# Returning routed rows by scatter and plain load in a mixture-of-experts stage on one Trainium2 core

## The chip, the cores and the metric

The kernel runs on one core of one Trainium2 chip. A core has a matrix engine (TensorE, PE in the profile; its weight loads are shown as PEld), a vector engine (VectorE, DVE), a scalar engine (ScalarE, ACT), a general engine (GpSimd, POOL), and a synchronizing engine (SyncE, SP) that here issues plain DMAs. Each engine runs its own instruction list in order; semaphores order the engines among each other. GpSimd issues the indirect DMAs, which take one row address per partition from a tile in on-chip memory.

The metric is the device time in microseconds (us) of one execution. Several executions give a median. One further execution is recorded by the hardware profiler, and every duration below comes from that one.

## The reference

The input is 2048 tokens (8 sequences of 256) of width 256, all in float32. There are three layers, each followed by a residual sum and a layer norm.

```python
x = _layernorm(x + attention(x))          # 16 heads of 64, causal
x = _layernorm(x + slot_attention(x, ctx))  # 3 rounds of attention on ctx and a GRU cell
# third layer: a mixture of 8 experts beside a shared one
router_probs = softmax(x @ gate_w + gate_b)
expert_values, expert_indices = top_k(router_probs, k=2)
expert_values = expert_values / (sum(expert_values) + 1e-09)
moe_out = sum over the 2 chosen experts of expert_value * mlp(x, ew1[e], eb1[e], ew2[e], eb2[e])
x = _layernorm(x + x + mlp(x, sh_w1, ...) + moe_out)
```

Every `mlp` is 256 to 1024 to 256 with a tanh-approximated GELU. The change lies in the third layer.

## The kernel before

**Blocks.** Tokens are held in four blocks of 512 (`X[i]`, token-major, four groups of 128 partitions; `XT[i]`, feature-major). The first two layers fill the first 650 us and are not altered, except that the tiles `X[i]` become wider.

**Routing.** For each block, `route_rest(i)` computes the gate, the two best experts (`hot1`, `hot2`), their weights (`wt1`, `wt2`) and running counts. `place(i)` turns them into row numbers `slots[0]` and `slots[1]` in a table `xd` in device memory (2048 rows for each expert, and 256 spare), and issues eight indirect DMAs on POOL (L901): each of four groups of 128 tokens is scattered to its first and its second expert's rows. `tables()` turns the counts into a list of 23 tiles: 16 of two groups of 128 rows (pairs), 7 of one. `tei` holds each tile's expert, `tri` its first row.

**Expert tiles.** For each tile, SP loads the rows (`tile_fetch`, L1124, which waits for all the scatters), the first expert matrix (`tile_weights`) and the second (`tile_weights2`); `tile_turn` transposes the rows on TensorE and copies them out of PSUM on VectorE; `tile_up` and `tile_down` do the two matrix products. `tile_down` adds the bias on VectorE into `yo`, and SP stores `yo` into the same rows of a second table `yd` (L1172). Both tables are filled with zeros by two large DMAs early in the second layer (L535).

**Shared units.** The shared expert is cut into eight units of 256 tokens, numbered 0 to 7: `shared_up(u)` (TensorE, then GELU on ScalarE) and `shared_down(u)`, a generator that `parts(u)` steps twice. Its last step adds the result to `Z[i]` on VectorE (called z4, z5, ... below after the unit's number). Units below `SHARED_FIRST` run before the expert tiles, in the time in which routing and scatters go on; the others run after the tiles.

**The tail.** After the last tile, `fetch_back(i)` gathers each token's two rows from `yd` with eight indirect DMAs on POOL for each block (L1182); `take_back(i)` does eight VectorE instructions `Z += wt * y` (L1196); `finish(i, ...)` is the layer norm of a block (statistics L221 and L222, the root on ScalarE L130 and L131, three small VectorE steps, scaling L239) and the store to the output (L1200).

**Order.** From L1257 on, PE, ACT, DVE and POOL execute in the order in which the program is written. In the tile stage this holds for PE and ACT; there the framework orders DVE, POOL and SP itself. The tail before is:

```python
    shared_up(4); fetch_back(0); shared_up(5); fetch_back(1); take_back(0)
    parts(4); take_back(1); shared_up(6)
    nc.scalar.preload_act_table_set(LNEXP)
    finish(0); finish(1); fetch_back(2); parts(5); shared_up(7)
    nc.scalar.preload_act_table_set(LNEXP)
    take_back(2); finish(2); fetch_back(3); next(part[6]); take_back(3); next(part[6])
    finish(3, 0, half)   # then unit 7's two halves, each with its add and finish
```

Of the kernel before, what the change touches and what calls it, by code (L numbers as in the profile page):

```python
# [47 lines left out]
SHARED_FIRST = 4  # L48

NY = 16  # L50
# [11 lines left out]
def decoder_kernel(  # L62
# [47 lines left out]
    X = [act.tile([P, NSUB, D], F32, tag=f"X{i}", name=f"X{i}") for i in range(NBLK)]  # L110
# [42 lines left out]
    xd = tc.dram_tile([ROWS, D], F32, name="xd")  # L153
    yd = tc.dram_tile([ROWS, D], F32, name="yd")
# [376 lines left out]
    zeros = b1.tile([P, D], F32, name="zeros")  # L531
    nc.gpsimd.memset(zeros, 0.0)

    for table in (xd, yd):
        nc.sync.dma_start(  # L535
            table.rearrange("(p r) d -> p r d", p=P), zeros.unsqueeze(1).to_broadcast([P, ROWS // P, D])
        )
# [284 lines left out]
    def route_rest(i):  # L822
# [28 lines left out]
        def best(src, k, hot):  # L851
            top, first = s(f"top{k}"), s(f"first{k}")
            nc.vector.tensor_reduce(top, src, AX.X, ALU.max)
            tt(hot, src, wide(top), ALU.is_equal)
            tt(hot, hot, rankb, ALU.mult)
            nc.vector.tensor_reduce(first, hot, AX.X, ALU.max)
            tt(hot, hot, wide(first), ALU.is_equal)
            return top

        blk = ts(i, NSUB)  # L860
        top1 = best(pb, 1, hot1[:, blk, :])
        rest = t("rest")
        nc.vector.scalar_tensor_tensor(rest, hot1[:, blk, :], -2.0, pb, ALU.mult, ALU.add)
        top2 = best(rest, 2, hot2[:, blk, :])
# [9 lines left out]


    puts = []

    def place(i):
# [19 lines left out]
        for n in range(NSUB):  # L898
            for slot in slots:
                g = i * NSUB + n  # L900
                put = nc.gpsimd.indirect_dma_start(  # L901
                    out=xd[:, :],
                    out_offset=bass.IndirectOffsetOnAxis(ap=slot[:, g : g + 1], axis=0),
                    in_=X[i][:, n, :],
                    in_offset=None,
                )
                if puts:
                    tc.declare_no_dep(put.ins, group="puts", reason="other rows")
                tc.add_to_no_dep_group("puts", put.ins)
                puts.append(put)  # L910

    def tables():
# [81 lines left out]
        nc.vector.tensor_scalar(te, te, float(NE - 1), None, ALU.min)  # L994
        tei = fr.tile([P, NTILE], I32, name="tei")
# [116 lines left out]
    TI = {}  # L1112
# [7 lines left out]
    def tile_fetch(t):  # L1120

        row = nc.sync.value_load(tri[0:1, t : t + 1], min_val=0, max_val=ROWS - RT)
        xg = f2.tile([P, 2, D], F32, tag="xg", name=f"xg_{t}", bufs=4)[:, 0 : groups(t), :]
        load = nc.sync.dma_start(xg, rows_of(xd, row, t))  # L1124
        for put in puts:
            tc.add_manual_dep(
                load.ins,
                put.ins.name,
                mybir.DependencyInfo(mybir.DependencyClass.Sync, mybir.DependencyReason.DATA),
                reason="rows of the table",  # L1130
            )
        TI[t] = [row, xg]

    def tile_weights(t):
# [8 lines left out]
        TI[t] += [w1_sb, w2_sb, bt, b2t, e]  # L1143

    def tile_weights2(t):

        row, xgT, w1_sb, w2_sb, bt, b2t, e = TI[t]
        nc.sync.dma_start(w2_sb, ew2[ds(e, 1), :, :].rearrange("e (c p) d -> p (e c) d", p=P))
        nc.sync.dma_start(b2t, b2[ds(e, 1), :].to_broadcast([P, D]))

    def tile_turn(t):
# [8 lines left out]
        TI[t][1] = xgT  # L1160

    def tile_up(t):
        row, xgT, w1_sb, w2_sb, bt, b2t, e = TI[t]
        HT["t", t] = up(w1_sb, bt, xgT, f"t{t}")

    def tile_down(t):
        row, xgT, w1_sb, w2_sb, bt, b2t, e = TI.pop(t)
        n = groups(t)
        po = down(w2_sb, HT.pop(("t", t)), f"t{t}", groups=n)
        yo = f2.tile([P, 2, D], F32, tag="yo", name=f"yo_{t}")[:, 0:n, :]  # L1170
        tt(yo, po[:, 0:n, :], b2t.unsqueeze(1).to_broadcast([P, n, D]), ALU.add)
        nc.sync.dma_start(rows_of(yd, row, t), yo)  # L1172
# [3 lines left out]
    def fetch_back(i):  # L1176

        for n in range(NSUB):
            for j, slot in enumerate(slots):
                g = i * NSUB + n  # L1180
                y = f2.tile([P, D], F32, tag="y", name=f"y_{g}_{j}", bufs=NY)
                nc.gpsimd.indirect_dma_start(  # L1182
                    out=y,
                    out_offset=None,
                    in_=yd[:, :],
                    in_offset=bass.IndirectOffsetOnAxis(ap=slot[:, g : g + 1], axis=0),
                )
                Y[g, j] = y

    def take_back(i):  # L1190

        for n in range(NSUB):
            g = i * NSUB + n
            for j, wt in enumerate((wt1, wt2)):
                z = Z[i][:, n, :]
                nc.vector.scalar_tensor_tensor(z, Y.pop((g, j)), wt[:, g : g + 1], z, ALU.mult, ALU.add)  # L1196
# [31 lines left out]
    for t in TILES[:2]:  # L1228
        tile_fetch(t)
    tile_weights(TILES[0])  # L1230
    tile_weights2(TILES[0])
    for u in range(2, SHARED_FIRST):
        shared_up(u)
        if u == SHARED_FIRST - 1:
            tile_fetch(TILES[2])
            tile_weights(TILES[1])
            tile_turn(TILES[0])
        parts(u)
    for u in range(SHARED_FIRST, nunit):
# [19 lines left out]
    shared_up(4)  # L1259
    fetch_back(0)  # L1260
    shared_up(5)
    fetch_back(1)
    take_back(0)
    parts(4)
    take_back(1)
    shared_up(6)
    nc.scalar.preload_act_table_set(LNEXP)
    for i in range(2):
        finish(i, 0, NSUB)
    fetch_back(2)  # L1270
    parts(5)
# [4 lines left out]
    fetch_back(3)  # L1276
    next(part[6])
    take_back(3)
    next(part[6])
# [74 lines left out]
```

## Time and profile before

| what | value |
|---|---|
| median of 3 runs | 1054.72 us (1053.62 to 1055.31) |
| the profiled execution's own time | 1057.97 us |
| its span | 1056.3 us, 13679 instructions |
| mean granted TensorE clock | 0.991 of full speed |
| PE busy | 1031.2 us |
| DVE, ACT, POOL busy | 484.3, 466.6, 257.4 us |

The span runs from the first to the last recorded instruction or transfer, so the execution's own time is 1.67 us longer. The stages on the time axis of the span: attention to about 373 us, slot attention to about 650 us, routing with shared units 0 to 3 to 714 us, expert tiles to 994 us, the tail to the end. Lines of the timeline give the start, the duration, the engine and source line, the operation with its output and inputs, the count of merged instructions, and in brackets the idle time of that engine before it with what ended it.

### The profile page before, as it was taken

The page shows a single profiled execution, that of the slowest core. Times are in us where ns is not written, and L with a number is a line of the kernel's source. Part 1 is how long each engine was busy: PE and PEld are TensorE (multiplying, and loading weights), DVE is VectorE, ACT ScalarE, POOL GpSimd, SP SyncE. Part 2 cuts the span into 40 slices and gives each one's busy share as a digit, 9 for nine tenths or more (in the row PEclk, how much of TensorE's full clock was granted, in tenths as well). Part 3 has the DMA queues.
Part 4 walks back from the last instruction along what each step waited for, and adds up shares of the span by engine and source line. Part 5 has one row for each costly group of instructions (what it writes and reads, how often), then busy time and mean ns, then how long its engine had stood idle before and what let it go on. Part 6 is the DMA issues. An engine that isn't in the chain of part 4 may idle for free. (4 is left out here: it accounts for less than half of the span.)

```text
span 1056.3 us, 13679 instructions
## 1 busy us (share of the span) xinstructions
PE 1031.2 (98%) x4686; PEld 714.5 (68%) x4686; DVE 484.3 (46%) x1378; ACT 466.6 (44%) x1156; POOL 257.4 (24%) x280
## 2 busy tenths in 40 slices
PE   9999999899898999999999999999999999999997
PEld 5444555455444865565655657888888888888886
DVE  4677766677678462444443568630110100101057
ACT  3567766665667123555545535223222222222232
POOL 2333423542367122112112003430000000000172
PEclk9999999899899999999999999999999999999999
DMA  9754434343345489990000001155766676665143
GB/s 325 122 86 83 83 67 74 60 76 68 68 90 102 118 286 348 348 311 1 1 0 1 1 0 44 63 167 194 253 208 237 205 255 213 221 223 171 64 120 105
DMA packets 195492, 144.24 MB, mean 137 GB/s; under 512 B 107551, under 2 KB 185951, under 8 KB 195423
## 3 DMA queue, kind: packets, MB, share of 16 engines
q1 hardware_dynamic: 191263, 132.88, 44.8%
q0 software_dynamic: 3072, 8.39, 2.5%
q10 hardware_dynamic: 1088, 2.10, 0.5%
q8 instruction: 37, 0.61, 0.2%
q14 instruction: 32, 0.26, 0.1%
HBM read 72.70 MB, written 45.48 MB: 112 GB/s over the span
## 5 line engine op out<-in xcount | busy, mean ns | idle before, releaser
L1063 ACT ACTIVATE hT_t<-ph_t,bt 128x256 f32<-128x256 f32 (+1 forms) x184 | 71.3, 438 | 202.6 <-issue 139.1
L348 ACT ACTIVATE sc<-sc,nmax 128x128 f32<-128x128 f32 (+1 forms) x256 | 113.3, 443 | 106.5 <-DVE nmax L335 106.2
L363 POOL TENSOR_TENSOR sc<-sc,sums 128x256 f32<-128x256 f32 (+1 forms) x128 | 104.0, 833 | 185.0 <-DVE sums L360 185.0
L1054 PE MATMUL ph_t<-xgT,w 128*128 128x256 f32 (+1 forms) x736 | 140.3, 348 | 0.8 <-ACT hT_t L1063 0.8
L1068 PE MATMUL pf_t<-w,hT_t 128*128 128x256 f32 x624 | 138.3, 379 | 0.0
L1054 PEld LDWEIGHTS ph_t<-xgT,w 128*128 128x128 f32 x736 | 123.8, 190 | 15.0 <-ACT hT_t L1063 1.0
L748 PE MATMUL gate<-XT,whh_sb 128*128 128x512 f32 x288 | 133.8, 593 | 0.0
L1068 PEld LDWEIGHTS pf_t<-w,hT_t 128*128 128x128 f32 x624 | 116.9, 190 | 15.0
L1182 POOL DMA_INDIRECT y<-yd,slot x32 | 31.0, 967 | 308.1 <-PE ph_s L1054 298.7
L748 PEld LDWEIGHTS gate<-XT,whh_sb 128*128 128x128 f32 x288 | 54.2, 189 | 48.5 <-issue 46.2
L391 DVE COPY pT<-turned 128x1536 uint16<-128x1536 uint16 x64 | 86.3, 1348 | 1.1 <-DMA turned<-planes 1.1
L335 DVE CUSTOM_DVE_ANT_0 sc<-pp,mask 128x128 f32<-128x128 f32 (+1 forms) x256 | 76.0, 353 | 19.5 <-PE pp L323 19.0
L757 PEld LDWEIGHTS gate<-at,G 120*128 120x128 f32 x288 | 54.5, 189 | 29.9 <-issue 23.2
L1159 DVE COPY xgT<-xg 128x512 f32<-128x512 f32 (+1 forms) x23 | 14.0, 611 | 131.7 <-PE xg L1157 131.7
L379 ACT COPY planes<-sc 128x1536 uint16<-128x1536 uint16 x48 | 70.5, 1470 | 5.9 <-POOL sc L363 5.8
L605 DVE TENSOR_TENSOR yo<-pf_t,b2t 128x512 f32<-128x512 f32 (+1 forms) x23 | 14.0, 610 | 127.9 <-PE pf_t L1068 127.9
L757 PE MATMUL gate<-at,G 120*128 120x256 f32 x288 | 72.2, 379 | 0.4 <-DVE at L605 0.4
L298 PE MATMUL pq<-XT,wq_sb 128*128 128x512 f32 x128 | 66.4, 643 | 0.0
L298 PE MATMUL pq<-XT,wk_sb 128*128 128x512 f32 x128 | 63.3, 617 | 0.0
L308 PE MATMUL pv<-wv_sb,XT 128*128 128x512 f32 x128 | 59.7, 594 | 0.0
L405 PE MATMUL po<-pT,v 128*64 128x256 f32 (+1 forms) x512 | 57.1, 345 | 1.0 <-DVE sums L360 1.0
L421 PE MATMUL py<-wo_sb,ot 128*128 128x256 f32 x256 | 57.9, 381 | 0.0
(209 smaller groups left out, 1430.9 us busy)
## 6 DMA issues: line engine op xcount, KB each, us to landing
w<-in_ew_dram SPq DMA_DIRECT2D x46, 1024.0 KB, 5.5
xd<-zeros SPq DMA_DIRECT2D x1, 16640.0 KB, 51.2
yd<-zeros SPq DMA_DIRECT2D x1, 16640.0 KB, 99.4
xg<-xd SPq DMA_DIRECT2D x16, 256.0 KB, 5.2
yd<-yo SPq DMA_DIRECT2D x16, 256.0 KB, 5.6
b2t<-in_b_dram SPq DMA_DIRECT2D x23, 128.0 KB, 5.2
sh<-in_sh_w_dram SPq DMA_DIRECT2D x2, 1024.0 KB, 6.7
X<-in_x_dram SPq DMA_DIRECT2D x3, 512.0 KB, 11.6
```

What stands on the lines that cost most here:

```text
L298: nc.tensor.matmul(pq, w[:, dc, ts(pr, P)], XT[i][:, dc, :], start=dc == 0, stop=dc == DC - 1)
L308: nc.tensor.matmul(pv, XT[i][:, dc, ts(n, P)], wv_sb[:, dc, ts(hf, 512)], start=dc == 0, stop=dc == DC - 1)
L335: nc.vector.tensor_tensor_reduce(out=sc[:, h, seg[t]], in0=pp[h][:, seg[t]], in1=mask[:, seg[t]], scale=-(HD**-0.5), scalar=3.0e38, op0=AL ...
L348: nc.scalar.activation(sc[:, h, seg[t]], sc[:, h, seg[t]], AF.Exp, scale=-1.0, bias=nmax[:, t, h : h + 1], accum_out=sums[:, t, h : h + 1],)
L363: nc.gpsimd.tensor_tensor(sc[:, :, seg[t]], sc[:, :, seg[t]], sums[:, t, :].unsqueeze(2).to_broadcast([P, 2, w]), ALU.mult,)
L379: nc.scalar.copy(planes, words)
L391: nc.vector.tensor_copy(pT.rearrange("p h c -> p (h c)").bitcast(U16).rearrange("p (n w) -> p w n", w=2), turned.rearrange("p (w c) q -> p ...
L748: nc.tensor.matmul(pg[:, oc, :], whh_sb[:, dc, o], XT[i][:, dc, :], start=dc == 0, stop=not given and dc == DC - 1,)
L757: nc.tensor.matmul(pg[:, oc, ts(bi, S)], G[:, BPB * i + bi, o], AT_[p][:, bi, :], start=not hidden, stop=not hidden or bi == BPB - 1,)
L1054: nc.tensor.matmul(ph[:, a, 0:w], w1_sb[:, dc, ts(c, P)], rhs[:, dc, :], start=dc == 0, stop=dc == DC - 1,)
L1063: nc.scalar.activation(hT[:, c, 0:w], ph[:, a, 0:w], AF.Gelu_apprx_tanh, bias=bias[:, c : c + 1])
L1068: nc.tensor.matmul(po, hT[:, c, ts(a, P)], w2_sb[:, c, :], start=c == 0, stop=c == FC - 1)
```

## The change

Tokens get an address of their own. The tiles `X[i]` become 16 columns wider (`XW`, row width `DW` = 272). Column 256 holds twice the token number plus 1; column 257 holds the rank of the token's first expert. The scatters into `xd` carry these columns along. In `tile_turn`, three small VectorE instructions make from them the row of the new table `yd` to which each result belongs: `2 * (token + 1) + j`, where j is 1 for the first expert and 0 for the second; unused rows of a tile go to rows of their own behind the tokens' rows. `tile_down` then issues one or two indirect DMAs on POOL in place of SP's store. `fetch_back(i)` is one plain load of 1 MB on SP, which waits for all these scatters. `yd` is not filled with zeros any more.

In `place`, a small `memset` of the last column of groups n and n+1 stands on POOL after the two scatters of group n. The scatters of group n read that column, so POOL waits for their end before it goes on with group n+1.

`SHARED_FIRST` goes from 4 to 5, the turning of the first tile comes after `parts` of the last early unit, and the tail is written anew.

```diff
-SHARED_FIRST = 4
+SHARED_FIRST = 5
+DW = D + 16
-    X = [act.tile([P, NSUB, D], F32, tag=f"X{i}", name=f"X{i}") for i in range(NBLK)]
+    XW = [act.tile([P, NSUB, DW], F32, tag=f"X{i}", name=f"X{i}") for i in range(NBLK)]
+    X = [t[:, :, 0:D] for t in XW]
...
-    xd = tc.dram_tile([ROWS, D], F32, name="xd")
-    yd = tc.dram_tile([ROWS, D], F32, name="yd")
+    xd = tc.dram_tile([ROWS, DW], F32, name="xd")
+    yd = tc.dram_tile([2 * (NT + 1) + P * (2 * NPAIRT + NSINGLE), D], F32, name="yd")
+    for i in range(NBLK):
+        nc.gpsimd.memset(XW[i][:, :, D:DW], 0.0)
+        nc.gpsimd.iota(XW[i][:, :, D], pattern=[[2 * P, NSUB]], base=2 * (i * BLK + 1), channel_multiplier=2, ...)
...
-    for table in (xd, yd):
-        nc.sync.dma_start(
-            table.rearrange("(p r) d -> p r d", p=P), zeros.unsqueeze(1).to_broadcast([P, ROWS // P, D])
-        )
+    nc.sync.dma_start(
+        xd.rearrange("(p r) d -> p r d", p=P), zeros.unsqueeze(1).to_broadcast([P, ROWS // P, DW])
+    )
...
-        top1 = best(pb, 1, hot1[:, blk, :])
+        top1 = best(pb, 1, hot1[:, blk, :], XW[i][:, :, D + 1])
...
                 put = nc.gpsimd.indirect_dma_start(
                     out=xd[:, :],
...
-                    in_=X[i][:, n, :],
+                    in_=XW[i][:, n, :],
...
+            if n + 1 < NSUB:
+                nc.gpsimd.memset(XW[i][:, n : n + 2, DW - 1 : DW], 0.0)
...
         nc.vector.tensor_copy(xgT, pt)
-        TI[t][1] = xgT
+        to = f2.tile([P, 2], I32, tag="to", name=f"to_{t}", bufs=6)
+        own, none = (f2.tile([P, 2], F32, tag=tag, name=f"{tag}_{t}")[:, 0:n] for tag in ("own", "none"))
+        g = 2 * t if n == 2 else NPAIRT + t
+        nc.vector.scalar_tensor_tensor(
+            own, xg[:, :, D + 1], tile_rank[:, t : t + 1], xg[:, :, D], ALU.is_equal, ALU.add
+        )
+        nc.vector.scalar_tensor_tensor(none, xg[:, :, D], 0.0, unused[:, g : g + n], ALU.is_equal, ALU.mult)
+        tt(to[:, 0:n], own, none, ALU.add)
+        TI[t][0:2] = to, xgT
...
-        yo = f2.tile([P, 2, D], F32, tag="yo", name=f"yo_{t}")[:, 0:n, :]
+        yo = f2.tile([P, 2, D], F32, tag="yo", name=f"yo_{t}", bufs=3)[:, 0:n, :]
         tt(yo, po[:, 0:n, :], b2t.unsqueeze(1).to_broadcast([P, n, D]), ALU.add)
-        nc.sync.dma_start(rows_of(yd, row, t), yo)
+        for k in range(n):
+            put = nc.gpsimd.indirect_dma_start(
+                out=yd[:, :],
+                out_offset=bass.IndirectOffsetOnAxis(ap=to[:, k : k + 1], axis=0),
+                in_=yo[:, k, :],
+                in_offset=None,
+            )
...
     def fetch_back(i):
-        for n in range(NSUB):
-            for j, slot in enumerate(slots):
-                g = i * NSUB + n
-                y = f2.tile([P, D], F32, tag="y", name=f"y_{g}_{j}", bufs=NY)
-                nc.gpsimd.indirect_dma_start(out=y, in_=yd[:, :], in_offset=... slot[:, g : g + 1] ...)
+        y = f2.tile([P, NSUB, 2, D], F32, tag="y", name=f"y_{i}")
+        load = nc.sync.dma_start(
+            y, yd[2 * (i * BLK + 1) : 2 * ((i + 1) * BLK + 1), :].rearrange("(n p j) d -> p n j d", p=P, j=2)
+        )
+        after(load, outs)
...
     tei, tri = tables()
-    for t in TILES[:2]:
-        tile_fetch(t)
+    tile_fetch(TILES[0])
     tile_weights(TILES[0])
     tile_weights2(TILES[0])
+    for t in TILES[1:3]:
+        tile_fetch(t)
     for u in range(2, SHARED_FIRST):
         shared_up(u)
-        if u == SHARED_FIRST - 1:
-            tile_fetch(TILES[2])
-            tile_weights(TILES[1])
-            tile_turn(TILES[0])
         parts(u)
+    tile_weights(TILES[1])
+    tile_turn(TILES[0])
...
-    shared_up(4)
-    fetch_back(0)
+    for i in range(2):
+        fetch_back(i)
     shared_up(5)
-    fetch_back(1)
-    take_back(0)
-    parts(4)
-    take_back(1)
     shared_up(6)
     nc.scalar.preload_act_table_set(LNEXP)
     for i in range(2):
+        take_back(i)
+        fetch_back(i + 2)
+    parts(5)
+    for i in range(2):
         finish(i, 0, NSUB)
-    fetch_back(2)
-    parts(5)
+    parts(6)
     shared_up(7)
     nc.scalar.preload_act_table_set(LNEXP)
     take_back(2)
     finish(2, 0, NSUB)
-    fetch_back(3)
-    next(part[6])
     take_back(3)
-    next(part[6])
     finish(3, 0, half)
```

The `y` tiles are two of 8 KB per partition where there were sixteen of 1 KB.

## The prediction, made before the changed kernel was run

> **What bounds the kernel now.** I read the page's busy times first, then TensorE's waits, then the timeline of the two places that the change touches: the start of the expert tiles and the tail.
>
> ```profile
> PE 1031.2 (98%) x4686; PEld 714.5 (68%) x4686; DVE 484.3 (46%) x1378; ACT 466.6 (44%) x1156; POOL 257.4 (24%) x280
> ```
>
> ```profile
> PE pp L321 <- DVE qk L300: 13.3, 11, 2.9
> ...
> PE ph_t L1054 <- ACT hT_t L1063: 0.8, 1, 0.8
> ```
>
> The first line is the page's, the others are TensorE's waits (total us, times, longest). TensorE is busy for 98% of the span. Only one line of waits is over 1.2 us in all, and it lies in attention, which the change leaves alone. In the tile stage TensorE waits once, for 0.8 us. So everything that the change takes off SP and POOL in the tiles was hidden, and TensorE's work is the same after as before: one shared unit moves from behind the tiles to ahead of them. A gain can come only from what follows TensorE's last product.
>
> ```profile
> 720.82 0.60 PE L1157 MATMUL xg<-ident,xg 128*128 128x128 f32 x4
> 721.45 0.69 DVE L1159 COPY xgT<-xg 128x512 f32<-128x512 f32 x1 [6.66 <-PE xg L1157]
> 722.24 7.14 PE L1054 MATMUL ph_t<-xgT,w 128*128 128x256 f32 x32 [0.83 <-ACT hT_t L1063]
> ```
>
> This is that one wait: the second tile is turned directly ahead of its own `tile_up`. The label names ACT, but the copy on DVE (721.45 to 722.14) is what ends last.
>
> ```profile
> 1008.06 7.07 PE L1068 MATMUL pf_s<-sh,hT_s 128*128 128x256 f32 x32
> ...
> 1015.17 0.69 DVE L605 TENSOR_TENSOR Z<-Z,pf_s 128x512 f32<-128x512 f32 x1 [4.89 <-PE pf_s L1068]
> 1015.77 3.23 DVE L1196 SCALAR_TENSOR_TENSOR Z<-y,wt,Z 128x256 f32<-128x256 f32 x7
> ...
> 1020.29 0.42 DVE L221 BATCH_NORM_STATS2 bnst<-Z 128x6 f32<-128x256 f32 x1
> ...
> 1026.70 0.41 DVE L221 BATCH_NORM_STATS2 bnst<-Z 128x6 f32<-128x256 f32 x1
> ...
> 1031.40 0.68 DVE L605 TENSOR_TENSOR Z<-Z,pf_s 128x512 f32<-128x512 f32 x1
> 1032.00 3.75 DVE L1196 SCALAR_TENSOR_TENSOR Z<-y,wt,Z 128x256 f32<-128x256 f32 x8
> 1035.67 0.42 DVE L221 BATCH_NORM_STATS2 bnst<-Z 128x6 f32<-128x256 f32 x1
> 1035.68 13.98 PE L1068 MATMUL pf_s<-sh,hT_s 128*128 128x256 f32 x64
> ...
> 1040.50 3.75 DVE L1196 SCALAR_TENSOR_TENSOR Z<-y,wt,Z 128x256 f32<-128x256 f32 x8
> ...
> 1044.16 0.68 DVE L605 TENSOR_TENSOR Z<-Z,pf_s 128x512 f32<-128x512 f32 x1
> ...
> 1047.88 0.41 DVE L605 TENSOR_TENSOR Z<-Z,pf_s 128x256 f32<-128x256 f32 x1
> ...
> 1050.48 0.41 DVE L605 TENSOR_TENSOR Z<-Z,pf_s 128x256 f32<-128x256 f32 x1
> ```
>
> This is the tail. Two things are to be seen. DVE runs in the written order: at 1015.17 it had waited 4.89 us for unit 4's product, with `take_back(1)` queued behind. And from 1020.29 DVE hardly pauses: `finish(0)`, `finish(1)`, z5, `take_back(2)`, and so on to 1053.16 (the last scaling). TensorE is done at 1049.66. So at the end two engines finish nearly together: TensorE through four units in 55.4 us (994.25 to 1049.66), DVE 3.5 us later. The gathers on POOL feed DVE, but after 1020 DVE is the slower of the two.
>
> **The change part by part, against the profiled execution (span 1056.3).**
>
> *Scatters in pairs.* The trace has no such wait. The nearest row is the scatter's own landing:
>
> ```profile
> xd<-X,slot POOLq DMA_INDIRECT x32, 2.4
> ```
>
> A pair takes 0.96 + 0.31 us up to the second scatter's start (rows of L901), then 2.4 us to land and about 0.3 us for the memset: 4.0 us. The last pair of a block has no wait (2.5 us). POOL starts `place(2)` at 679.5 as before; twice 3 x 4.0 + 2.5 ends at 708.5, the last lands near 710. SP's first fetch waits for that, as does the first tile's load of weights behind it: fetch at about 710, landed after 5.4 us (L1124's median; longest 7.8) at 716 to 718; weights issued by 713, landed by 722 even with the longest landing of L1141 (9.0). TensorE needs the rows after three units: 685.76 + 3 x 13.86 = 727.3 (a unit is half of 713.91 - 685.76 - 0.44). Cost: 0, and 9 us of cover. The six waits decide only if each landing takes 1.5 us more (3.9; the longest in the trace is 3.6). The second tile's weights, now behind `parts(4)` in the program, stand behind two more fetches on SP and issue by 716, 18 us ahead of their use. `place(0)` and `place(1)` end by about 653 and 675, ahead of POOL's next work. The Trainium skill speaks against the wider rows: "DMA: Bandwidth & Descriptors", section "How a descriptor splits into AXI transactions", says that a transfer that does not begin on a 256-byte boundary fetches unused bytes. Rows of 1088 bytes begin 0, 64, 128 or 192 bytes off, so a row takes some 37 beats for 32, an estimate of 16% more: landing 2.8 for 2.4, fetch 6.3 for 5.4. No row here shows it, and with it the rows arrive 3 us later, still under cover; the sum is the same by both.
>
> *First tile turned behind `parts(4)`.* A new wait on TensorE: before, 6.9 us of unit 3 lay over the copy. Lower bound 0.83 us (the row above); upper bound 1.5, if DVE does z4 (0.60 to the next start) in full ahead of the copy: z4 starts 0.2 after the product, the copy at 0.8, TensorE at 1.6, less 0.44 of transposes that existed before. I take 1.15. Behind the copy, three small DVE instructions (near 0.2 us each) are before `yo`; DVE is busy 26.7 of 279 us in the tile stage, so they cost nothing, and neither does the one added to `tables()`, which ends at 693, before the scatters.
>
> *Results scattered.* 39 indirect DMAs on POOL (16 x 2 + 7) of 1.27 us each stand in an engine that is idle for 298.7 us there; SP loses 23 stores and the waits for `yo` ahead of its weight loads. TensorE had no wait for weights, so the gain is 0; if POOL fell behind, three `yo` tiles (some 30 us) would cover it.
>
> *Zeros.* 16.6 MB are not written, 1.0 MB are added. They run from 373 to 473 us; TensorE is busy for 100.55 of the 101 us from 374 to 475: 0.
>
> *Start.* Eight small POOL instructions; POOL idles 10.8 us there. If the first loads of `X` had to wait for them, up to 2.4 us would be lost. I take 0: two loads into interleaved columns of `wq_sb` leave 1.1 us apart though each takes 4 us to land, so the order is kept by columns, not by whole tiles.
>
> *The tail.* Let E be TensorE's end of the tiles: 994.25 now, 994.25 + 13.86 + 1.15 = 1009.3 after. From E: the last `yo` 0.2 to 0.9, two scatters, the second landed at about 4.8; a load of 1 MB takes 5.5 (row of `w`), so block 0 is there at 10.3, block 1 at about 13.3. Two `take_back` (3.7 each) end by 18.7. Then DVE stands before z5 until TensorE has done units 5 and 6 up and 5 down: E + 20.9, exactly as z4 now (1015.17 - 994.25). From there, with durations from start to start in the rows above:
>
> z5 0.60; `finish(0)` and `finish(1)` 4.70 each (1026.70 to 1031.40); z6 0.60; `take_back(2)` 3.67; `finish(2)` 4.83 (1035.67 to 1040.50); `take_back(3)` 3.66; `finish(3, 0, half)` 3.01 (1044.87 to 1047.88); unit 7's halves 2.60 and 2.68. Sum 31.05.
>
> DVE therefore ends at E + 51.95, while TensorE has only three units and ends at E + 41.6. The overhang behind TensorE grows from 3.5 to 10.4 us: the moved unit was the cover of `finish(0)` and `finish(1)`, and those still come after a wait for TensorE. Last instruction 1009.3 + 51.95 = 1061.2, and the output's landing as before (1056.3 - 1053.16 = 3.1): span 1064.4, 8.1 us more. The profiled time would be 1057.97 + 8.1 = 1066.1. The median of the runs is 3.25 under the profiled time; I carry the difference over: 1054.72 + 8.1 = 1062.8.
>
> *The gathers gone.* A second rule weighs here. Of DVE's passes, eight `take_back` instructions beside gathers took 3.75 us (1032.00) and eight without any (1040.50, POOL done at 1038.6) took 3.75 too. The Trainium skill, "GPSIMD Engine Reference", section "Key points", says that GpSimd shares its SBUF interfaces with VectorE, in contention with instructions of two SBUF inputs, which these are. By the rule, each of some 15 gathers after 1020.3 could hold DVE for up to its 0.95 us, and without them DVE would gain up to 14 us (an estimate), enough to turn the sign. By the row the gain is 0, and I take the row. What is seen to stretch is the gather (1.13 for 0.95).
>
> **The rivals.**
>
> *A, DVE sets the end as above:* 1062.8, own range 1060.5 to 1065.5. Chance 0.76.
>
> *B, also a late supply:* scatters or loads land later than their rows. At the first tile this takes 9 us of lateness; in the tail `take_back(1)` has only 2.2 us of slack before z5, so 4 us more there, from 23 tiles' scatters and two loads of 1 MB at once, puts 2 us on top, and a late first tile more: 1064 to 1070. Against it: longest landings of 3.6 and 9.0. Chance 0.10.
>
> *C, the wait for z5 does not bind:* DVE does the two `finish` before z5, from E + 17.7. Then z5 follows at E + 27.1, and the rest (31.05 - 9.40) ends at E + 48.9: 5 us more than before, 1059.7. Against it: the 4.89 us wait before z4 shows the written order. Chance 0.05.
>
> *D, not slower:* DVE's own instructions get shorter because POOL leaves the shared interface. Place: the 31 us from z5 on. It decides from 8.1 us on, a quarter of that chain; then TensorE's end plus 2.8 sets the time, 1054.72 + 1.15 - 0.7 = 1055.2, and any further gain has to come from shorter waits in the first layers. Against it: 3.75 with gathers, 3.75 without. Chance 0.09 with all unseen causes of that kind.
>
> **How the numbers follow.** The prediction is A's 1062.8. The range runs from C's neighbourhood to the lower half of B: 1059.5 to 1066.5. About 0.2% (2.1 us) is what a measurement of this kernel can tell from no change. A, B and C lie over it; D gives 0.05 to no difference and 0.04 to faster.
>
> **What would show it.** Right: TensorE's last product near E + 41.6 with DVE's last scaling 10 us behind; DVE idle 2 us ahead of z5; `finish(0)` starting after z5; POOL empty in the tail; one new TensorE wait of about 1.2 us before the first tile; the last scatter of `place(3)` near 710. Wrong: `take_back` or the statistics shorter than 0.48 and 0.40 us; TensorE idle before the first tile for several us; block 1 landing after E + 17.

## The result, and the profile after

The changed kernel took 1062.67 us against 1054.87 us for the kernel before in the same comparison: ratio 1.0072, 95% interval 1.0054 to 1.0091. It is slower by 7.8 us; 8.1 had been forecast. One of the five executions of the changed kernel took 2748.68 us; it is left out of the ratio, and its cause is not known. The profiled execution took 1062.67 us, its span is 1061.0 us.

Two marks make the two traces comparable: the first product of `place(1)`, and E, TensorE's end of the tiles. In the trace of before they are

```profile
656.29 0.30 PE L884 MATMUL place<-cur,upper 128*128 128x32 f32 x2
994.25 13.98 PE L1054 MATMUL ph_s<-XT,sh 128*128 128x256 f32 x64
```

and in the trace of after

```profile
653.31 0.30 PE L902 MATMUL place<-cur,upper 128*128 128x32 f32 x2
1006.29 13.98 PE L1089 MATMUL ph_s<-XT,sh 128*128 128x256 f32 x64
```

(the row of E is the first product behind the tiles). The first mark comes 2.98 us earlier in the trace of after. This is not the change's doing: slot attention already begins 2.96 us earlier (370.21 against 373.17), behind attention, in which the granted clock was 0.97 between 150 and 200 us and between 250 and 300 us where it was 0.93 in the trace of before. It also shows that leaving out 16.6 MB of zeros behind that point gave nothing that can be seen. From that mark to E it is 337.96 us before and 352.98 after; from E to the end of the span 62.05 before and 54.71 after. So +15.02 and -7.34, together +7.7 us.

The start of the tiles, from the timeline of after (start, duration, engine and line, operation, and in brackets the engine's idle time before it with what ended it):

```profile
717.35 7.07 PE L1103 MATMUL pf_s<-sh,hT_s 128*128 128x256 f32 x32
724.25 0.60 PE L1186 MATMUL xg<-ident,xg 128*128 128x128 f32 x4
724.46 0.69 DVE L615 TENSOR_TENSOR Z<-Z,pf_s 128x512 f32<-128x512 f32 x1 [4.17 <-PE pf_s L1103]
725.06 0.68 DVE L1188 COPY xgT<-xg 128x512 f32<-128x512 f32 x1
725.80 7.17 PE L1089 MATMUL ph_t<-xgT,w 128*128 128x256 f32 x32 [0.94 <-DVE xgT L1188]
```

The first tile is now turned behind unit 4's second product. VectorE is asked for z4 and for the copy at once, does z4 first, and TensorE waits 0.94 us. It is the only wait over 0.3 us that TensorE has gained behind the first mark; the 0.8 us ahead of the second tile are as before.

The tail, from the timeline of after:

```profile
1016.96 7.42 DVE L1242 SCALAR_TENSOR_TENSOR Z<-y,wt,Z 128x256 f32<-128x256 f32 x16 [9.77 <-DMA y<-yd]
1027.22 0.69 DVE L615 TENSOR_TENSOR Z<-Z,pf_s 128x512 f32<-128x512 f32 x1 [2.83 <-PE pf_s L1103]
1027.82 0.42 DVE L232 BATCH_NORM_STATS2 bnst<-Z 128x6 f32<-128x256 f32 x1
...
1041.08 7.07 PE L1103 MATMUL pf_s<-sh,hT_s 128*128 128x256 f32 x32
...
1046.22 3.75 DVE L1242 SCALAR_TENSOR_TENSOR Z<-y,wt,Z 128x256 f32<-128x256 f32 x8
...
1057.76 0.41 DVE L250 TENSOR_SCALAR Z<-Z,mv,rstd 128x256 f32<-128x256 f32 x1
```

E is 1006.29. VectorE is done with both first `take_back` at 1024.4 and stands idle for 2.83 us until TensorE has produced z5 at E + 20.9. Behind that wait lie `finish(0)` (from 1027.82), `finish(1)` and all the rest. TensorE ends its last unit at 1048.15 (E + 41.9), VectorE at 1058.2 (E + 51.9): 10 us lie behind TensorE's last product, where there were 3.5 before.

### The profile page after: what moved, and what is told of

Same layout as the page of the kernel before. It is cut to its first block, busy times and chain, and to the rows that moved or that the text cites. A ratio compares the mean times of both kernels' runs of the same rounds, so it can differ in the third digit from the quotient of the medians.

```text
span 1061.0 us, 13689 instructions
## 1 busy us (share of the span) xinstructions
PE 1027.9 (97%) x4686; PEld 711.8 (67%) x4686; DVE 493.1 (46%) x1448; ACT 466.6 (44%) x1156; POOL 266.9 (25%) x308
## 5 line engine op out<-in xcount | busy, mean ns | idle before, releaser
L1214 POOL DMA_INDIRECT yd<-yo,to x39 | 37.4, 959 | 271.3 <-DVE yo L615 266.5
L346 DVE CUSTOM_DVE_ANT_0 sc<-pp,mask 128x128 f32<-128x128 f32 (+1 forms) x256 | 76.0, 353 | 18.7 <-PE pp L334 18.2
L1193 DVE SCALAR_TENSOR_TENSOR own<-xg,tile_rank 128x2 f32<-128x2 f32 (+1 forms) x23 | 5.1, 221 | 123.8 <-DMA xg<-xd 123.8
## 6 DMA issues: line engine op xcount, KB each, us to landing
X<-in_x_dram SPq DMA_DIRECT2D x3, 512.0 KB, 11.9
```

The source lines that it names most:

```text
L346: nc.vector.tensor_tensor_reduce(out=sc[:, h, seg[t]], in0=pp[h][:, seg[t]], in1=mask[:, seg[t]], scale=-(HD**-0.5), scalar=3.0e38, op0=AL ...
```

## The experiments

Two theories were to be told apart. **A**, the prediction's: VectorE's written order in the tail sets the end; the fifth early unit is missing there as cover. **S**, formed after the first experiments: where GpSimd issues many indirect DMAs without a gap, the other engines run out of instructions.

The experiments ran on a chip (chip 2 in the results) on which the kernel before is slower: 1092 us in the first two sets, 1086 in the last. Whether the comparison above ran on the same chip is not recorded. So each kernel is compared with the kernel before in its own set, and by ratios with the unaltered changed kernel below. The traces of one set are single executions, so small differences between them count only where a wait in the trace accounts for them. Expectations of the first two sets know only theory A and what could stand against it then.

**The changed kernel, unaltered, on that chip**

> The changed kernel itself, beside the kernel before on one chip. Theory A: some 8 us slower (ratio 1.0072 in the first measurement). In the first set of experiments the kernel before took 1092 us where it had taken 1055, and the four variants 1064 to 1072 with one stall of 5 to 6 us of TensorE in unit 2's product that the first trace of the changed kernel does not have. If that set's chip only adds that stall to all kernels, the changed kernel is 1072 to 1073 there, so that its four variants lie 2.7, 0.9, 8 and 3.7 us lower as theory A has them.

Measured: 1071.54 us, ratio to the kernel before 0.9819 (0.9802 to 0.9837). The sign is turned: here the change is 1.8% faster. All ratios below are to be held against this 0.982. TensorE stops once that it did not in the first comparison, in the second product of unit 2:

```profile
698.68 6.20 PE L1103 MATMUL pf_s<-sh,hT_s 128*128 128x256 f32 x20 [4.84 <-ACT hT_s L1098]
```

**The kernel before, unaltered, one execution**

> The kernel before, for its trace on the chip of this set. If this chip is like the one of the first measurement: the trace as before, 1053 to 1058. If it is like the one of the first set of experiments: near 1092, and the trace shows TensorE waits of some 30 us in all that name what the kernel before does there and the variants do not; candidates are the second table's zeros (16.6 MB on the queue from 373 to 473 us) and the start of the expert tiles.

Measured: 1089.53 us, span 1087.8. TensorE's waits in this trace, those with the shared units' products (total, times, longest):

```profile
PE ph_s L1054 <- issue: 11.7, 8, 2.2
PE ph_s L1054 <- ACT hT_s L1063: 11.1, 3, 10.0
```

Neither line is in the trace of before that the prediction used. "issue" means that the engine waited for nothing that the profile shows. The timeline of the same trace shows where:

```profile
692.51 1.99 PE L1054 MATMUL ph_s<-XT,sh 128*128 128x256 f32 x8 [0.92 <-ACT hT_s L1063]
704.51 3.78 PE L1054 MATMUL ph_s<-XT,sh 128*128 128x256 f32 x8 [10.00 <-ACT hT_s L1063]
...
1039.16 0.58 PE L1054 MATMUL ph_s<-XT,sh 128*128 128x256 f32 x1 [1.52 <-issue]
1041.25 0.59 PE L1054 MATMUL ph_s<-XT,sh 128*128 128x256 f32 x1 [1.51 <-issue]
1043.35 0.59 PE L1054 MATMUL ph_s<-XT,sh 128*128 128x256 f32 x1 [1.51 <-issue]
```

The first stop ends 2.9 us after the 16 scatters of `place(2)` and `place(3)`, which GpSimd issued from 681.6 to 701.6 with 0.3 us between them; after it eight products take 3.78 us, about as long as sixteen did at 687.89 (3.70). The granted clock tells why: 1.00 there, 0.50 between 704.5 and 708.3. The second lies in the run of 24 gathers from 1013.7 to 1043.5: single products, 1.5 us apart. GpSimd keeps its rhythm meanwhile:

```profile
1040.08 0.95 POOL L1182 DMA_INDIRECT y<-yd,slot  x1 [0.30 <-issue]
1041.34 0.95 POOL L1182 DMA_INDIRECT y<-yd,slot  x1 [0.30 <-issue]
1042.59 0.95 POOL L1182 DMA_INDIRECT y<-yd,slot  x1 [0.30 <-issue]
```

The windows 653 to 715 us of the trace of before and of this one (columns: length, then busy time and count for PE, PEld, DVE, ACT, POOL, the granted clock, DMA share, GB/s):

```profile
653.00:715.00 62.00, 61.65 (x320) 54.42 (x320) 31.67 (x165) 17.51 (x40) 23.80 (x24) 1.00 0.34 112
```

```profile
653.00:715.00 62.00, 49.93 (x236) 42.98 (x235) 28.87 (x158) 13.31 (x30) 23.81 (x24) 0.86 0.24 79
```

GpSimd has done the same 24 operations in both. TensorE has done 84 products fewer, ScalarE 10 instructions fewer. That gave theory S.

**finish(0) and finish(1) ahead of unit 5's second product**

```diff
-    parts(5)
     for i in range(2):
         finish(i, 0, NSUB)
+    parts(5)
     parts(6)
```

> The changed kernel with finish(0) and finish(1) written ahead of parts(5). Theory A (VectorE's order sets the end: two finishes wait behind z5, and z5 waits for TensorE): VectorE goes on from E + 18.1 instead of E + 20.9, the rest of its chain is the same 31 us, so the end comes about 2.7 us earlier, near 1060.0, and the idle time of 2.8 us ahead of z5 is gone. Rival B (the time was lost at the start of the tiles, by the wider rows, the scatters or the new TensorE wait, and the tail follows TensorE): no change, 1062.7. Rival C (the late landing of the rows in the tail sets the end): no change either.

Measured: 1069.24 us, ratio 0.9792 (0.9768 to 0.9817). Against 0.9819 that is -0.0027, no more than the two intervals allow by chance. The trace decides better: VectorE's last scaling ends at E + 51.3 instead of E + 51.9, so the edit is worth 0.6 us, not 2.7. The line that took the rest, from this kernel's timeline:

```profile
1047.27 0.39 DVE L232 BATCH_NORM_STATS2 bnst<-Z 128x6 f32<-128x256 f32 x1
...
1051.47 1.38 DVE L250 TENSOR_SCALAR Z<-Z,mv,rstd 128x256 f32<-128x256 f32 x4
```

Between the last statistics of `finish(2)` and its scaling lie 3.8 us, where the changed kernel needs 1.4 (1043.11 plus 0.39, to 1044.92). The root comes from ScalarE, and there it stands behind unit 7's GELU and the reload of the table, which follow each other without a gap:

```profile
1048.16 0.84 ACT L1098 ACTIVATE hT_s<-ph_s,vec_sb 128x256 f32<-128x256 f32 x2 [0.89 <-PE ph_s L1089]
1049.02 1.28 ACT L1317 ACT_TABLE_LOAD   x1
1050.31 0.30 ACT L131 ACTIVATE rstd<-mv,eps_ln 128x4 f32<-128x4 f32 x1
```
The wait for z5 is gone, and the next wait in the written order has taken its place.

**The first tile turned earlier**

```diff
     for u in range(2, SHARED_FIRST):
         shared_up(u)
+        if u == SHARED_FIRST - 1:
+            tile_weights(TILES[1])
+            tile_turn(TILES[0])
         parts(u)
-    tile_weights(TILES[1])
-    tile_turn(TILES[0])
```

> The changed kernel with the first tile turned ahead of parts(4), as before it was turned ahead of parts(3). Theory A: the TensorE wait of 0.94 us before the first tile goes, everything behind it moves forward by as much, near 1061.7. If the tail's end hung on something that does not move with TensorE's end of the tiles: no change. If the rows were not yet there at that point, TensorE would wait longer than before.

Measured: 1071.54 us, ratio 0.9816 (0.9794 to 0.9838). The wait for `xgT` of 0.94 us is gone from TensorE's waits, but the wait in unit 2, which only this chip has, was 6.0 us in this trace and 4.8 in that of the unaltered kernel. A gain of 0.9 us in the time cannot be seen beside that.

**Four units first, four last**

```diff
-SHARED_FIRST = 5
+SHARED_FIRST = 4
...
+    shared_up(4)
     shared_up(5)
+    take_back(0)
+    fetch_back(2)
+    parts(4)
+    take_back(1)
+    fetch_back(3)
     shared_up(6)
     nc.scalar.preload_act_table_set(LNEXP)
     for i in range(2):
-        take_back(i)
-        fetch_back(i + 2)
+        finish(i, 0, NSUB)
     parts(5)
-    for i in range(2):
-        finish(i, 0, NSUB)
-    parts(6)
     shared_up(7)
...
     finish(2, 0, NSUB)
+    next(part[6])
     take_back(3)
+    next(part[6])
```

Scatters, plain loads and pairs stay as in the change.

> Scatters, pairs, wide rows and plain loads kept, but the moved unit put back: SHARED_FIRST = 4, and the tail in the order of the kernel before (unit 4's two steps at their old places). Theory A: VectorE again has the old chain under four units of TensorE, so the tail takes about 62 us from E as before, and only the wait of about 1 us before the first tile is left: 1055 to 1056.5, some 7 us under the changed kernel. Rival B (scatters, wide rows and loads cost the time themselves): stays near 1062. A gain by the loads themselves would show as less than 1054.

Measured: 1063.76 us, ratio 0.9746 (0.9722 to 0.977): 0.7% below the unaltered change, about 8 us. In the trace E comes 11.9 us earlier after the mark (347.83 for 359.71), and the tail is 7.0 us longer (61.73 for 54.72), with TensorE ending 3.5 us ahead of VectorE as before. That leaves 4.9 us in the traces; the stop in unit 2 happened to cost 2.0 us more in this one (22.6 us for the unit, against 20.6), and without that the gain is 6.9 us, as theory A has it. So, as far as one execution of each can show it, the place of the fifth unit accounts for the loss that the prediction put on it.

**Half of take_back(2) and take_back(3) left out**

This kernel leaves out the first expert's part in blocks 2 and 3.

```diff
-            for j, wt in enumerate((wt2, wt1)):
+            for j, wt in enumerate((wt2, wt1) if i < 2 else (wt2,)):
```

> The changed kernel without the first expert's part in take_back(2) and take_back(3): eight VectorE instructions of 0.46 us from start to start are left out, so blocks 2 and 3 lack that part of the sum. Theory A: all of it is on the path that sets the end, 3.7 us less, near 1059.0. Rivals B and C: VectorE has slack there, no change.

Measured: 1068.63 us, ratio 0.9783 (0.9763 to 0.9804), 0.0036 below the unaltered change, about 3.9 us with an uncertainty of about 3. From E to the end of the span the trace shows 2.5 us less (52.23 for 54.72) where two cuts of 2.1 us were made: VectorE's chain sets the end, but the cut in `take_back(2)` is mostly lost in the same wait for ScalarE's root as above (the scaling of `finish(2)` starts at E + 38.3 for E + 38.6).

**The changed kernel without the pairs**

```diff
-            if n + 1 < NSUB:
-                nc.gpsimd.memset(XW[i][:, n : n + 2, DW - 1 : DW], 0.0)
```

> The changed kernel without the memset between the pairs of scatters. Theory A: POOL is done with place(3) some 4 to 9 us earlier, TensorE does not notice (its first tile comes 20 us later): as the changed kernel, within 1 us. If the pairs were what costs the time: several us less. If scatters that follow each other without a pause disturb the other engines: longer, with TensorE waits at 675 to 700 us.

Measured: 1084.87 us, ratio 0.9939 (0.992 to 0.9958): 1.2% above the unaltered change. A was wrong here: this kernel loses about 13 us by the ratio and 11.5 in the traces. From the mark to E it takes 371.16 us instead of 359.71, and the tail is the same (54.66 for 54.72). TensorE's waits and the timeline:

```profile
PE ph_s L1086 <- issue: 9.6, 2, 8.6
```

```profile
692.32 1.99 PE L1086 MATMUL ph_s<-XT,sh 128*128 128x256 f32 x8 [0.93 <-issue]
702.94 3.78 PE L1086 MATMUL ph_s<-XT,sh 128*128 128x256 f32 x8 [8.63 <-issue]
```

It is the stop of the kernel before, at the same place, in a kernel without gathers. Without the pauses GpSimd issues 16 scatters from 681.4 to 701.4. Not all of the 11.5 us is this stop: 4.7 us are lost ahead of unit 2, where the granted clock was 0.70 between 664 and 674 us. A kernel with its pauses in place shows such a dip too (0.66, in the experiment with all 16 in pairs below), so that part may not be the pauses' doing.

**The kernel before with five units first, gathers kept**

```diff
-SHARED_FIRST = 4
+SHARED_FIRST = 5
...
-    shared_up(4)
-    fetch_back(0)
     shared_up(5)
+    fetch_back(0)
     fetch_back(1)
-    take_back(0)
-    parts(4)
-    take_back(1)
     shared_up(6)
     nc.scalar.preload_act_table_set(LNEXP)
+    take_back(0)
+    take_back(1)
+    parts(5)
     for i in range(2):
         finish(i, 0, NSUB)
     fetch_back(2)
-    parts(5)
+    parts(6)
     shared_up(7)
...
     fetch_back(3)
-    next(part[6])
     take_back(3)
-    next(part[6])
```

> The kernel before, gathers kept, with only the unit moved: SHARED_FIRST = 5, the first tile turned ahead of parts(4), three units in the tail. Theory A: the 32 gathers take 40 us on POOL from E + 4, VectorE's chain gets its last rows near E + 46 and ends near E + 57.6, where it ended at E + 58.9 with E one unit (13.9 us) earlier: some 12 us slower than the kernel before, so the scatters and loads are worth some 5 us once the unit is moved. Rival B (the unit's place is indifferent, the scatters cost): as the kernel before.

Measured: 1110.67 us, ratio 1.0181 (1.0157 to 1.0205). The moved unit costs even more here: against the kernel before on this chip, the way from the mark to E grows by 17.3 us (372.88 for 355.58), and the tail, which on one unit less should shrink, grows by 5.2 (83.21 for 77.98), where theory A's chain would have shortened it by about 1. TensorE loses more in the run of gathers than the kernel before does (11.7 us in 8 waits):

```profile
PE pf_s L1068 <- issue: 20.6, 11, 2.2
```

Why the same run costs more here is not shown.

**All 16 scatters of place(2) and place(3) in pairs**

In the changed kernel `place(3)`'s scatters fill `place(2)`'s pauses (see below), so pauses are missing where they would matter. This kernel holds them apart:

```diff
+                if i == 3 and pause:
+                    tc.add_manual_dep(put.ins, pause[-1].ins.name, ... NoSync ...)
...
-            if n + 1 < NSUB:
-                nc.gpsimd.memset(XW[i][:, n : n + 2, DW - 1 : DW], 0.0)
+            if n + 1 < NSUB or i == 2:
+                p = nc.gpsimd.memset(XW[i][:, n : min(n + 2, NSUB), DW - 1 : DW], 0.0)
+                if i == 2:
+                    pause.append(p)
```

> The changed kernel with place(3)'s scatters held behind place(2)'s last memset, so that all 16 go in pairs with a pause behind each pair (in the changed kernel place(3)'s scatters filled place(2)'s pauses, and GpSimd had no gap over 0.3 us but two short memsets for some 15 us). Theory A (the written order of the tail is all that counts): 8 pairs of 4.5 us from about 678 to 681 end at 714 to 717, the first fetch lands at 723 to 726 for a turn at about 724, so 0 to 2 us slower than the changed kernel, and TensorE's wait in the second unit is no shorter than before. Theory S (an unbroken run of indirect DMAs on GpSimd longer than some 12 us starves the other engines of instructions): the 4.8 us wait of pf_s in the second unit is gone, at most 2 us come back at the turn: 2 to 5 us faster than the changed kernel on a chip where that wait was there (1067 to 1070 if the kernel before takes 1092 there), and no gain where it was not.

Measured: 1069.08 us, ratio 0.9823 (0.9798 to 0.9849), no different from the unaltered change. The wait of `pf_s` is gone, as S says. But the last scatter starts at 715.2, and a new wait takes its place:

```profile
735.10 8.80 PE L1099 MATMUL ph_t<-xgT,w 128*128 128x256 f32 x32 [6.91 <-DVE xgT L1198]
```

The rows landed in time for the transposes (727.59). What was late is VectorE's copy: in the framework's order it stood behind z4, and z4 behind the small instructions on the rows of the fourth fetched tile, whose fetch was issued at 725.66 behind weights of 3 MB and landed at 733.4. The fetches started later because the pairs ended later, so each VectorE instruction that waits for one became late as well. In the times, cost and gain cancel; in this trace the way from the mark to E is 4.2 us longer than in that of the unaltered change, and 3.3 us of this lie ahead of unit 2, where the granted clock dipped to 0.66 between 664 and 674 us although TensorE did not stop.

**24 scatters a second time in the tail, without a gap**

```diff
     tile_down(TILES[-1])
+    for i in range(3):
+        put_again(i)      # place(i)'s eight scatters again, behind the last result scatter
```

> The changed kernel with 24 of place's scatters issued a second time behind the last result scatter, back to back (the same rows with the same content, after all fetches of xd; nobody waits for them). Theory A: GpSimd is idle there and nobody waits; 24 x 136 KB beside the 1 MB fetches may make the first block up to 1 us later, against 2.2 us of cover: within 1 us of the changed kernel. Theory S: the run lasts 24 x 1.26 = 30 us, TensorE runs dry 12 to 18 us after its start, that is from about E + 20, and loses 8 to 18 us in the tail in waits labelled issue; 5 to 15 us slower than the changed kernel on a chip of that kind.

Measured: 1087.79 us, ratio 1.0007 (0.9991 to 1.0023): about 1.9% above the unaltered change, 16 to 20 us, for DMAs that nobody waits for. ("remote" marks a wait ended by a semaphore event that the profile ties to no instruction of this core.) From the timeline of this kernel:

```profile
1039.23 0.59 PE L1103 MATMUL pf_s<-sh,hT_s 128*128 128x256 f32 x1 [1.51 <-issue]
1039.56 0.96 POOL L1249 DMA_INDIRECT xd<-X,slot  x1 [0.31 <-issue]
1040.64 0.58 PE L1103 MATMUL pf_s<-sh,hT_s 128*128 128x256 f32 x1 [0.82 <-issue]
...
1045.53 8.80 PE L1103 MATMUL pf_s<-sh,hT_s 128*128 128x256 f32 x28 [0.82 <-issue]
1047.85 0.69 DVE L615 TENSOR_TENSOR Z<-Z,pf_s 128x512 f32<-128x512 f32 x1 [18.64 <-remote]
```

E is 1009.84 here, the run lasts from 1013.5 to 1044.3, and z5 comes at E + 38.0 instead of E + 20.9. TensorE's products follow each other again from 1.2 us after the end of the run, at first slowly: the granted clock is 0.50 between 1045.5 and 1049.5.

**The same 24 scatters in pairs**

```diff
...
+                    behind[-1].ins.name,
...
+            behind.append(nc.gpsimd.memset(XW[i][:, n : min(n + 2, NSUB), DW - 1 : DW], 0.0))
```

> The same 24 scatters a second time, but in pairs, each pair followed by a memset that waits until the pair has been read (about 4.5 us a pair, 54 us in all, ending at about E + 59, past the end of the rest, so GpSimd itself may end the span some 5 us later). Theory A: no waits on TensorE; up to 5 us longer only because GpSimd's last pairs end last. Theory S: the same; no wait on TensorE labelled issue over 1 us in all, although the work is the same as in the unbroken run. So the two runs of 24 must differ on TensorE by S and not by A.

Measured: 1090.81 us, ratio 1.0034 (1.0018 to 1.0049). This time says only that GpSimd's last pairs end behind all else, at 1081.3. For TensorE and VectorE the tail is that of the unaltered kernel:

```profile
1014.87 13.98 PE L1089 MATMUL ph_s<-XT,sh 128*128 128x256 f32 x64
...
1028.68 13.98 PE L1103 MATMUL pf_s<-sh,hT_s 128*128 128x256 f32 x64
...
1035.79 0.69 DVE L615 TENSOR_TENSOR Z<-Z,pf_s 128x512 f32<-128x512 f32 x1 [2.69 <-PE pf_s L1103]
```

GpSimd in the same stretch:

```profile
1030.98 0.10 POOL L1263 MEMSET X<- 128x2 f32 x1 [1.67 <-DMA xd<-X,slot]
1031.73 0.96 POOL L1249 DMA_INDIRECT xd<-X,slot  x1 [0.65 <-POOL X L1263]
1033.00 0.96 POOL L1249 DMA_INDIRECT xd<-X,slot  x1 [0.30 <-issue]
```

z5 at E + 20.9, VectorE's last scaling at E + 52.0, no wait of TensorE in the tail. The same 24 scatters with the same rows: with about 2 us or more between the pairs (63 us for all) they cost TensorE nothing, without a gap (31 us) they cost 17 us. This shows, on this chip, that it is the dense run that stops the other engines, not the work in it. That it is instructions which they lack is inferred: TensorE's waits name nothing that it waited for ("issue"), and VectorE and ScalarE stop with it while GpSimd keeps its rhythm.

**Four last, with take_back(2) moved ahead**

The edit against the kernel with four units last:

```diff
+    take_back(2)
     for i in range(2):
         finish(i, 0, NSUB)
     parts(5)
     shared_up(7)
     nc.scalar.preload_act_table_set(LNEXP)
-    take_back(2)
     finish(2, 0, NSUB)
```

> The kernel with four units first and four last (as tried), and in its tail take_back(2) moved ahead of finish(0) and finish(1), into VectorE's idle time while ScalarE still has gelus to do. By theory A VectorE's 3.75 us leave the chain behind the last gelu, but TensorE's end (E + 55.9) is then the bound: its last group is followed by a chain of 2.7 us instead of 3.5 us, so 0.8 us faster than that kernel: ratio to the kernel before 0.974 if this is the chip on which it was 0.9746, about 1.000 on a chip where the change is 0.7 % slower. Theory S says nothing else: the stall in the second unit stays, 4 to 6 us on TensorE.

Measured: 1064.56 us, ratio 0.9786 (0.976 to 0.9811), against 1063.76 and 0.9746 without the move; the kernel before was 5 us faster in this set, so the ratios of the two sets differ by more than the times. In the traces VectorE's last scaling ends at E + 59.6, with the move, and at E + 58.9 without. The miss has the cause found above: with `take_back(2)` gone from its place, `finish(2)` reaches ScalarE's root sooner and waits for it (scaling at 1049.33, last statistics at 1044.18), and `take_back(3)` stands behind it. The root even comes later than without the move: `take_back(2)` holds up the roots of `finish(0)` and `finish(1)`, and unit 7's GELU, which follows them on ScalarE, begins at E + 37.7 instead of E + 36.5. In this execution the stop in unit 2 was 3.2 us (5.5 without the move), and the first tile waited 5.1 us for VectorE (0.95).

The kernel with four units last is the best of those run, 0.9746 of the kernel before on that chip. It did not run where the change was 0.7% slower. Its way from the mark to E without the stop in unit 2 (347.8 less 8.7) and its tail of 61.7 us would put it within about 1 us of the kernel before there; that is an estimate and was not measured.

The marks side by side (us, from the profiled executions):

| kernel | mark to E | E to the end |
|---|---|---|
| before, first comparison | 337.96 | 62.05 |
| after, first comparison | 352.98 | 54.71 |
| before, chip 2 | 355.58 | 77.98 |
| after, chip 2 | 359.71 | 54.72 |
| after, no pairs | 371.16 | 54.66 |
| after, four last | 347.83 | 61.73 |
| after, all 16 in pairs | 363.92 | 54.67 |
| before, five first | 372.88 | 83.21 |
| after, 24 scatters more, no gap | 358.16 | 71.76 |

The change has the two parts of the prediction on both: a unit more ahead of the tiles, a shorter tail. On chip 2 the old kernel pays 17.6 us more from the mark to E and 15.9 more in the tail than in the first comparison; the changed kernel pays 6.7 and nothing. The difference of the differences, 26.8 us, turns +7.7 into -19.1. Of the 17.6 us, 13.2 lie in unit 2 with its stop; 4.2 lie ahead of it, with the granted clock at 0.68 between 664 and 674 us, and the dip of the clock in the kernel with all 16 in pairs leaves it open whether these belong to the scatters.

## Why the prediction was right, and where it was not

**The unit and the new wait.** Predicted 13.86 + 1.15 = 15.01 us from the mark to E; measured 15.02. The moved unit took 13.81 us. From the turn to TensorE's next product it is 1.55 us, less the 0.44 that the transposes took before: 1.11 us where 1.15 was taken, of which the profile shows 0.94 as waiting. The order behind it was as reckoned: z4 0.2 us after the product, the copy 0.6 us after that.

**The tail.** Predicted E + 10.3 for the first block's landing, E + 18.7 for the end of the two `take_back`, E + 20.9 for z5, E + 51.95 for VectorE's end, E + 41.6 for TensorE's. Measured: 10.7, 18.1, 20.9, 51.9, 41.9. The chain of 31.05 us held because every link was read from the trace of before, and because ScalarE, which the sum did not follow, came in time by 0.34 us:

```profile
1043.76 0.30 ACT L131 ACTIVATE rstd<-mv,eps_ln 128x4 f32<-128x4 f32 x1 [0.34 <-DVE mv L233]
```

That part was luck. It was luck too that the comparison met none of the stops: on chip 2 the same two kernels lie 20 us apart the other way, far outside the range, for a cause that the prediction does not have.

**Rival C's price was wrong.** It put 3 us on the two `finish` going ahead of z5. The first experiment did just that and gained 0.6 us. The sum followed VectorE alone; `finish(2)` has a second condition, ScalarE's GELU of unit 7 and the table load behind it, and in the changed kernel this was met just in time, as the row above shows.

**Pairs.** The pauses were predicted at 4.0 us a pair and measured at 4.5 where they are real (the memset started 1.6 us after the second scatter, and the next scatter 0.6 after the memset). `place(3)` was predicted to end at 708.5 and ended at 701: the framework put its scatters into the pauses of `place(2)`, whose memsets then waited for nothing. The timeline of after shows it: the memset follows at once where it waited 1.6 us elsewhere, and the next scatter 0.28 us behind it where it was 0.6:

```profile
687.61 0.96 POOL L919 DMA_INDIRECT xd<-X,slot  x1 [0.30 <-issue]
688.58 0.12 POOL L932 MEMSET X<- 128x2 f32 x1
688.97 0.97 POOL L919 DMA_INDIRECT xd<-X,slot  x1 [0.28 <-POOL X L932]
```

In the first comparison this cost and gained nothing, as predicted. The experiments on chip 2 show a value of the pauses that the prediction did not see: up to 13 us, of which some 7 are the longer stop in unit 2.

**Wider rows.** By the Trainium skill's "DMA: Bandwidth & Descriptors", section "How a descriptor splits into AXI transactions", the estimate was a landing of 2.8 us and a fetch of 6.3 us. The scatters landed in 2.4 us as before (medians); the fetch of 272 KB took 6.0 against 5.2 for 256 KB. So the fetch lengthened by about the 16% of the estimate, the scatter did not, and both lay under cover. That the rows' beginnings are the reason was not tested.

**Scattered results.** Taken to land in 2.4 us; the median over the tiles is 6.0, beside the weight loads. In the tail it is 2.4, and only there does anybody wait for it.

**The gathers gone.** The prediction weighed a gain of up to 14 us on VectorE by the Trainium skill's "GPSIMD Engine Reference", section "Key points", against a row that showed none, and took 0. In the first comparison the row was right: `take_back` is 3.75 us before and after, so the contention that the section states did not show in these instructions. Rival D's sign came true on chip 2, but not by its mechanism: VectorE's instructions are no shorter there (eight in 3.75 us from 1048.34 in the kernel before, too). They come later, as do TensorE's and ScalarE's, which fits a late supply of instructions. Nothing in the trace of before, where GpSimd issued 32 gathers in 40 us without any such stop, could have shown it.

## What to carry to other kernels

Work that is moved off the end also takes away the cover of what stays there: follow the in-order engine from its last forced wait to the end, link by link, and ask at each link which other engine could become the second condition; a forecast from VectorE's links alone priced one reordering at 2.7 us that was worth 0.6. Where GpSimd issues many indirect DMAs in a row beside busy engines (runs of 16 and 24 stopped them here), put gaps between them (about 2 us behind each pair sufficed) or use plain loads, and look for waits labelled issue or remote on several engines at once. Repeat a comparison in which a result of 1% decides on more than one chip, or at another time.

## What the runs showed of the hardware

Beside an unbroken run of indirect DMAs at one in 1.26 us, TensorE, ScalarE and VectorE came to a stop on chip 2, it seems for lack of instructions: some 13 us after a run of 16 scatters began, and within about 10 to 20 us of the beginning of a run of 24 (TensorE's first gap at 1023.2 where the run began at 1013.5, and at 1030.7 where it began at 1013.7). In the run of 24 TensorE got single instructions at distances of about 0.7, 1.4 or 2.1 us until the run ended. A run broken only by short memsets, in the changed kernel (682.4 to 697.9 in its trace on chip 2), stopped TensorE too, for 3.2 to 6.0 us in the eight traces that have it. The DMA records of the instruction queues do not show how: the larger one moved 37 packets in 0.2% of the DMA engines' time, on chip 2 as in the first comparison. Why the same runs (16 scatters, 32 gathers) left no mark in the trace of before stays open, as does whether the chip or its condition differed.

After a stop of 10 us TensorE ran at half rate for about 4 us (eight products in 3.78 us where sixteen took 3.70, at a granted clock of 0.50), so the stop cost some 12. Stops of under 2 us had no such end: the eight products behind the wait of 0.92 us took 1.99 us.
